# Transformer block: GpSimd's order written out in the input stages, with three steps of the input work moved

## The chip, the cores and the metric

The kernel runs on one core of a Trainium2 chip. Its time is the device time of one execution in microseconds; lower is better. The core has five engines that run their own instruction streams and wait for each other by semaphores: TensorE (PE in the profile; its weight loads are PEld), VectorE (DVE), ScalarE (ACT), GpSimd (POOL) and SyncE (SP, which here only issues DMAs). Everything is in 32-bit floats.

## The reference

One block of a conditioned transformer (DiT) on x of 2 batches x 2048 tokens x 576 features, 16 heads of 36 features, hidden width 2304:

```
mod = silu(c) @ w_ada + b_ada                 # six rows of 576 a batch
xn  = ln(x) * (1 + sc_msa) + sh_msa
q, k, v = split(xn @ w_qkv + b_qkv)           # by head
q, k = ln(q) * qn_g + qn_b, ln(k) * kn_g + kn_b      # over a head's 36 features
x   = x + g_msa * (softmax(q k^T / 6) v @ w_proj + b_proj)
xn2 = ln(x) * (1 + sc_mlp) + sh_mlp
out = x + g_mlp * (gelu(xn2 @ w1 + b1) @ w2 + b2)
```

## The kernel before, in words

The work is in stages. For each batch: the input stage (`inputs`, q, k and v of 16 tiles of 128 tokens), attention (`attend`, 8 pairs of heads x 4 blocks of 512 queries x 4 groups of keys), and the output product (`outputs`). Then the two products of the MLP for both batches.

**Order.** The program is traced once, and a planner gives each engine an order: of the instructions that its own timing model takes for ready, the one that was written first goes first. Inside `tc.manual_schedule(engines=...)` the named engines keep the order in which the code is written. TensorE is fixed throughout; in `inputs`, VectorE and SyncE are fixed, GpSimd and ScalarE are not. Each engine then runs its order strictly: an instruction that waits holds up all behind it, and on GpSimd this includes the DMAs that it issues.

**One token tile t on its way.** Its rows are loaded into one of three buffers (`tile_loaded`, L980, a DMA on GpSimd's queue), normed on VectorE (`rows_normed`; one step, the standard deviation L276, is on ScalarE) and transposed in 32x32 squares (L996); four DMAs on GpSimd's queue (L1001) write these to DRAM so that they lie by feature. Three DMAs on GpSimd's queue (L1009 once, L1011 twice) read the tile back by feature into `xnt`, which has three buffers: tile t+2 takes the one that tile t-1 had, so TensorE must have finished with it. ScalarE scales and shifts it (L1018 four times for the first 512 features; L388 and L389 for the last 64). L388 writes the last chunk rounded to the short matmul format, L389 writes it in full to the buffer `tail`, and GpSimd subtracts one from the other (L390). I call that subtraction **the remainder of tile t**. A product takes the 576 columns in two halves; of each, four full chunks come first (L1098, eight rows in the profile, since a 32-bit matmul is two instructions) and then the two parts of the last chunk (L1100). So a tile's first product waits for the remainder at its second L1100, some 2 us after it has begun.

**After the products.** `biased` (L1112 for q and k, L1115 for v) adds the bias from PSUM; `squared` (L1051, ScalarE) and `head_scale` (reduction L1056 and reciprocal L1061 on VectorE, square root L1059 on ScalarE, the scaling L1063 `both` on GpSimd) norm q and k by head. `by_feature(t)` transposes a tile's q and k in squares (L1076) and writes them with four DMAs of SyncE (L1078) to DRAM. `take_k_block` reads k of four tiles back for the first pair of heads (L812, L814, SyncE), and L847, L856, L857 on VectorE make `km` and `ke` of it for attention.

**The loop of `inputs`.** Step t calls, in the order of the code: `begun(t)` (loads the rows of tile t+4 and the features of tile t+2), the products of q and k, `turned_ahead(t)` (norms tile t+3 and writes its squares), `head_scale(t - 1)`, the product of v, `by_feature(t - 2)`, `squared(t)`, and `modulated_ahead(t)` (L1018 to L390 for tile t+1). In batch 0, tiles 0, 1 and 2 come another way before the loop (`first_modulated`, and transposes on TensorE in `second_by_feature`), their q and v products come before the loop too, and there `bias_made` centres the bias by head, writes it to DRAM (L955, GpSimd) and reads it back spread over 128 partitions (L956, GpSimd). Tile 15 is worked after the loop.

`s` tiles (PSUM, two banks each) are four, so a product may stand three products long before its bias is added.

Of the kernel before, what the change touches and what calls it, by code (L numbers as in the profile page):

```python
# [8 lines left out]
F32 = mybir.dt.float32  # L9
# [7 lines left out]
P = 128  # L17
# [14 lines left out]
def dit_block(  # L32
# [25 lines left out]
    nc = tc.nc  # L58
# [315 lines left out]
    def part_tiles(pool, cols, **bufs):  # L374

        return (
            pool.tile([P, FULL, cols], F32, name="xnt", **bufs),
            pool.tile([P, 2, cols], F32R, name="xnt4", **bufs),
            pool.tile([P, P], F32, name="tail", bufs=1),
        )  # L380

    def affine(which, k, b):
# [369 lines left out]
    def block_of_small():  # L752
# [163 lines left out]
        def first_weights(then):  # L916

            pool, (wq, wq4, bq), close = weight_tiles()
            raw = pool.tile([64, 3 * C], F32, name="raw_rows")

            def columns(f0, n):
                f = slice(f0, f0 + n)
                nc.sync.dma_start(out=wq[:, :, f], in_=w_qkv[0:512, f].rearrange("(k p) f -> p k f", p=P))

            columns(2 * C, HALF)
            nc.sync.dma_start(out=raw, in_=w_qkv[512:576, :])
            columns(2 * C + HALF, HALF)
            then(1)
            columns(0, HALF)
            then(2)  # L930
            columns(HALF, HALF)
            nc.sync.dma_start(out=bq[:, 2 * C :], in_=b_qkv[2 * C :].partition_broadcast(P))
            columns(C, HALF)
            columns(C + HALF, HALF)

            def made(w):
                for a in range(2):
                    centred(wq[:, :, w * C + a * HALF : w * C + (a + 1) * HALF])

            def ends_made(w):  # L940
                part = slice(w * C, (w + 1) * C)
                if w < 2:
                    centred(raw[:, part].unsqueeze(1))
                weight_parts(wq4[:, part], raw[:, part])

            by_head = pool.tile([2 * H, HD], F32, name="by_head")
            nc.gpsimd.dma_start(out=by_head, in_=b_qkv[0 : 2 * C].rearrange("(h d) -> h d", d=HD))

            def bias_made():
                mean = pool.tile([2 * H, 1], F32, name="mean")  # L950
                nc.vector.tensor_reduce(mean, by_head, AX.X, ALU.add)
                nc.vector.tensor_scalar_mul(mean, mean, 1.0 / HD)
                nc.vector.tensor_scalar(by_head, by_head, mean, None, ALU.subtract)
                saved["bq"] = dram.tile([2 * C], F32, name="bq_kept")
                nc.gpsimd.dma_start(out=saved["bq"].rearrange("(h d) -> h d", d=HD), in_=by_head)  # L955
                nc.gpsimd.dma_start(out=bq[:, 0 : 2 * C], in_=saved["bq"].partition_broadcast(P))  # L956

            def kept():
                saved["wq"] = dram.tile([P, FULL, 2 * C], F32, name="wq_kept")
                saved["wq4"] = dram.tile([P, 3 * C], F32, name="wq4_kept")  # L960
                nc.sync.dma_start(out=saved["wq"], in_=wq[:, :, 0 : 2 * C])
                nc.sync.dma_start(out=saved["wq4"], in_=wq4.bitcast(F32))

            return (wq, wq4, bq), close, (made, ends_made, bias_made, kept)

        def kept_weights():
            _, (wq, wq4, bq), close = weight_tiles()
# [62 lines left out]
        def second_by_feature(rows):  # L1030
            xnt = part_tiles(xs["pool"], P, bufs=3)
            t4, t1 = transposed(*rows)
            modulated_parts(xnt, slice(0, P), t4, t1[:, :P], 0, 0)
            return xnt
# [6 lines left out]
        def inputs(b, weights, making, work, xnts, turned, loaded):  # L1041

            wq, wq4, bq = weights
# [22 lines left out]
            by_square = qk_rows["dram"].rearrange("(k d) (t g j) -> t g d k j", d=SQ, g=P // SQ, j=SQ)  # L1066
            NSQ = C // SQ

            def by_feature(t, w0=0, w1=2, ready=True):

                begun = [*taken] if ready else []
                if ready:
                    taken.clear()
                part = slice(w0 * C, w1 * C)
                turned_qk = work.tile([P, 2 * C], F32, name="turned_qk", bufs=3)
                nc.vector.transpose(turned_qk[:, part], both[t][:, part])  # L1076
                for g in range(P // SQ):
                    nc.sync.dma_start(  # L1078
                        out=by_square[t, g][:, w0 * NSQ : w1 * NSQ, :],
                        in_=turned_qk[g * SQ : (g + 1) * SQ, part].rearrange("p (k j) -> p k j", j=SQ),  # L1080
                    )
                for do in begun:
                    do()
                if t == TPB - 1 and w0 == 0:
                    taken.extend(take_q(0, 0))
                if t + 1 in key_tiles and w1 == 2:
                    i = key_tiles.index(t + 1)
                    taken.append(take_k_block(*key_tiles[i - 1 : i + 1]))

            def product(w, t, ps=None, steps=(0, 1)):  # L1090

                ps = ps or s_tile()
                full, parts, _ = xnts[t]
                for a in range(2):
                    f = slice(w * C + a * HALF, w * C + (a + 1) * HALF)
                    out_a = ps[:, a, :HALF]
                    for k in range(FULL) if 0 in steps else ():
                        nc.tensor.matmul(out_a, full[:, k, :], wq[:, k, f], start=k == 0, stop=False)  # L1098
                    for i in range(2) if 1 in steps else ():
                        nc.tensor.matmul(out_a, parts[:, i, :], wq4[:, f], start=False, stop=i == 1)  # L1100
                return ps
# [20 lines left out]
            def begun(t):  # L1122
                if t + 4 < NT:
                    loaded[t + 4] = tile_loaded(x[b, (t + 4) * P : (t + 5) * P, :], nc.gpsimd)
                if t + 2 < NT and t + 2 not in xnts:
                    xnts[t + 2] = input_loaded(turned.pop(t + 2), nc.gpsimd)

            def turned_ahead(t):
                if t + 3 in loaded:
                    turned[t + 3] = tile_turned(loaded.pop(t + 3), nc.gpsimd)  # L1130

            def modulated_ahead(t):
                if t + 1 < NT and t + 1 not in modulated:
                    input_modulated(b, xnts[t + 1])
# [1 line left out]
            modulated = {0}  # L1136
            done = 0
            if b == 0:
                made, ends_made, bias_made, kept = making
                done, modulated = 3, {0, 1, 2}  # L1140
                ends_made(2)
                rows = {t: tile_normed(loaded.pop(t)) for t in (1, 2)}
                chosen = rows_chosen(work)
                bias_made()
                v = two_steps(2, 0)
                biased(2, v, 0)
                made(0)
                xnts[1] = second_by_feature(rows[1])
                v = product(2, 1)
                biased(2, v, 1)  # L1150
                ends_made(0)
                xnts[2] = second_by_feature(rows[2])
                v = product(2, 2)
                biased(2, v, 2)
                gains_by_row(chosen)
                turned_ahead(0)
                made(1)
                ends_made(1)
                for t in range(done):
                    q = two_steps(0, t) if t == 0 else product(0, t)  # L1160
                    biased(0, q, t)

            for t in range(NT - 1):
                begun(t)
                if t >= done:
                    q = product(0, t)
                k = product(1, t) if t >= done else two_steps(1, t)
                if t >= done:
                    biased(0, q, t)
                turned_ahead(t)  # L1170
                biased(1, k, t)
                if t > 0:
                    head_scale(t - 1)
                if t >= done:
                    v = product(2, t)
                    biased(2, v, t)
                if b == 0 and t == TPB + 1:
                    kept()
                if t >= 2:
                    by_feature(t - 2)  # L1180
                squared(t)
                modulated_ahead(t)

            t = NT - 1
            k, q, v = (product(w, t) for w in (1, 0, 2))
# [5 lines left out]
            by_feature(t - 1)  # L1191
            biased(0, q, t)
            squared(t, 0, 1)
            by_feature(t, 1, 2)
            head_scale(t, 0, 1)
            biased(2, v, t)
            by_feature(t, 0, 1, ready=False)
# [220 lines left out]
        weights, close_weights, making = first_weights(row_loaded)  # L1418
        row_loaded(3, nc.gpsimd)
        for b in range(B):  # L1420
            work, close_work = opened("work", side="right")
            with tc.manual_schedule(engines={mybir.EngineType.DVE, mybir.EngineType.SP}):
                left = inputs(b, weights, making, work, xnts, turned, loaded)
            close_weights()
            close_work()
# [464 lines left out]
```

## Time and profile before

| | |
|---|---|
| median of 3 runs | 3172.99 us (3171.32 to 3174.12) |
| the profiled execution: its time, its span | 3172.15 us, 3170.4 us |
| granted TensorE clock, mean | 0.996 |
| TensorE busy | 3129.0 us of the span (99%) |
| VectorE, ScalarE, GpSimd busy | 1513.7, 1471.7, 660.8 us |
| input stage of batch 0 on TensorE | 19.2 to 247.8 us |
| input stage of batch 1 on TensorE | 1106.7 to 1319.8 us |
| one step of the input stage on TensorE (87.58 to 100.81) | 13.23 us |

In a timeline's row stand the start and the length in us, the engine, the line, the operation, out<-in and the number of instructions that the row merges; in brackets the idle time of the engine before it and what ended that. A DMA's row on POOL is the time that GpSimd takes to issue it; the landing comes later. "PE x <- y" in a list of waits is who waited for whom: us in total, times, longest. In the chain of work that ended last, a DMA's row lasts from its issue to its landing, and SPq is SyncE's time to issue.

### The profile page before, as it was taken

Reading aid. Unit: us, or ns where it says so; the run is one execution under the profiler, and the core shown is the slowest. Engines: PE = TensorE matmul, PEld = TensorE weight load, DVE = VectorE, ACT = ScalarE, POOL = GpSimd, SP = SyncE. Lnnn points to the kernel's source line nnn. Section 1 sums busy time; section 2 is a strip of 40 time slices with the busy share of each in tenths; the row PEclk is TensorE's granted clock in tenths of the full one; section 3 lists DMA queues with packets and bytes.
Section 4 is the critical chain, followed back from the end, with each engine's and each line's share of the span. In section 5 each row is a group of like instructions: output and inputs, shape, how many; then the busy total and the mean of one; then the engine's idle time right before and its main releaser. Section 6 shows DMA issues by size and latency. Waiting matters only on the chain.

```text
span 3170.4 us, 46708 instructions
## 1 busy us (share of the span) xinstructions
PE 3129.0 (99%) x17553; PEld 1863.7 (59%) x17553; DVE 1513.7 (48%) x2173; ACT 1471.7 (46%) x2843; POOL 660.8 (21%) x924
## 2 busy tenths in 40 slices
PE   7999999999999999999999999999999999999999
PEld 5874333333333787633333333358888888777777
DVE  6653344444444556433444344345566554445454
ACT  2225666666666122366666666643565552000000
POOL 4541000111110455300001111012333320112121
PEclk9999999999999999999999999999999999999999
DMA  5654211222221745511122212246545434333331
GB/s 157 148 110 99 76 45 55 67 73 75 69 69 44 216 109 117 99 44 37 42 56 76 78 58 74 59 143 196 162 133 138 132 109 158 117 121 112 120 105 39
DMA packets 304531, 311.94 MB, mean 98 GB/s; under 512 B 183464, under 2 KB 237096, under 8 KB 302184
## 3 DMA queue, kind: packets, MB, share of 16 engines
q1 hardware_dynamic: 256704, 192.78, 21.3%
q0 software_dynamic: 44048, 110.48, 13.4%
q10 hardware_dynamic: 3544, 5.60, 0.5%
q8 instruction: 141, 2.31, 0.3%
q14 instruction: 94, 0.77, 0.1%
HBM read 191.80 MB, written 106.45 MB: 94 GB/s over the span
## 4 chain that ended last, share of the span: by engine, by line
PE 89%; DMA 2%; DVE 1%; issue 1%; POOL 1%; SPq 1%; ACT 0%; POOLq 0%; DVEq 0%; ACTq 0%
PE b L1233 29%; PE b L1220 19%; PE s L1802 15%; PE m L1642 11%; PE s L1098 6%; PE s L406 3%; PE m L1656 2%; PE one L1642 2%; PE s L1100 1%; DMA qk<-turned_qk 0%; PE s L417 0%; DMA ke<-qk 0%; DMA xnt<-turned 0%; POOL both L1063 0%; SPq L1078 0%
## 5 line engine op out<-in xcount | busy, mean ns | idle before, releaser
L1224 ACT ACTIVATE pt<-b 128x512 f32<-128x512 f32 x2048 | 1057.4, 610 | 490.6 <-PE b L1233 278.9
L1233 PE MATMUL b<-pt,vt 128*64 128x512 f32 x4096 | 937.0, 599 | 0.0
L1233 PEld LDWEIGHTS b<-pt,vt 128*64 128x64 f32 x4096 | 272.3, 137 | 584.7 <-issue 442.5
L1220 PE MATMUL b<-qm,km 32*128 32x512 f32 x4096 | 572.1, 616 | 2.8 <-issue 2.5
L1283 DVE TENSOR_TENSOR ot<-b,ot 128x512 f32<-128x512 f32 x192 | 132.8, 692 | 628.3 <-PE b L1233 628.3
L1220 PE MATMUL b<-qe,ke 16*128 16x512 f32 x2048 | 423.7, 792 | 2.1 <-DVE ke L857 2.1
L1098 PE MATMUL s<-wq,xnt 128*128 128x288 f32 x1536 | 405.3, 407 | 2.5 <-ACT xnt L395 2.1
L1220 PEld LDWEIGHTS b<-qm,km 32*128 32x128 f32 x4096 | 192.1, 185 | 277.4 <-ACT pt L1224 211.2
L1802 PE MATMUL s<-ws,as 128*128 128x288 f32 x1440 | 351.8, 406 | 0.0
L1098 PEld LDWEIGHTS s<-wq,xnt 128*128 128x128 f32 x1536 | 281.8, 190 | 65.3 <-ACT xnt L395 1.6
L1802 PEld LDWEIGHTS s<-ws,as 128*128 128x128 f32 x1440 | 273.6, 190 | 75.6
L1252 DVE RECIPROCAL den<-den 128x512 f32<-128x512 f32 x64 | 213.6, 3337 | 9.7 <-DMA den<-den_dram 9.7
L1642 PE MATMUL m<-xnt,wb 128*128 128x256 f32 x864 | 210.3, 379 | 2.1 <-DVE cs L1676 1.2
L1642 PE MATMUL m<-s,wb 128*128 128x256 f32 x864 | 210.0, 379 | 0.0
L1001 POOL DMA_DIRECT2D turned<-squares x212 | 142.7, 679 | 256.2 <-DVE squares L996 234.7
L1281 DVE COPY ot<-b 128x512 f32<-128x512 f32 x64 | 44.3, 692 | 281.6 <-PE b L1233 281.6
L1220 PEld LDWEIGHTS b<-qe,ke 16*128 16x128 f32 x2048 | 107.9, 185 | 118.2 <-issue 112.8
L1642 PEld LDWEIGHTS m<-s,wb 128*128 128x128 f32 x864 | 164.2, 190 | 22.3
L1642 PEld LDWEIGHTS m<-xnt,wb 128*128 128x128 f32 x864 | 158.9, 190 | 21.6 <-DVE cs L1676 1.4
L1680 ACT ACTIVATE cs<-cs,b_sb 128x512 f32<-128x512 f32 x144 | 98.9, 719 | 112.2 <-DVE cs L1675 86.2
L812 POOL DMA_DIRECT2D km<-qk x56 | 27.9, 499 | 582.1 <-PE b L1220 573.5
L1018 ACT ACTIVATE xnt<-xnt,mod 128x128 f32<-128x128 f32 x244 | 100.4, 481 | 96.8 <-DMA xnt<-turned 96.8
(204 smaller groups left out, 2937.0 us busy)
## 6 DMA issues: line engine op xcount, KB each, us to landing
gelu<-cs SPq DMA_DIRECT2D x144, 256.0 KB
hidden<-gelu SPq DMA_DIRECT2D x16, 2304.0 KB
x_dram<-spare POOLq DMA_DIRECT2D x64, 288.0 KB, 2.5
qk<-turned_qk SPq DMA_DIRECT2D x120, 144.0 KB
qm<-qk SPq DMA_DIRECT2D x256, 64.0 KB
den<-den_dram SPq DMA_DIRECT2D x128, 128.0 KB
turned<-squares POOLq DMA_DIRECT2D x212, 72.0 KB, 2.5
xnt<-turned POOLq DMA_DIRECT2D x54, 256.0 KB, 3.9
```

Of the source, the lines that this page charges most:

```text
L406: nc.tensor.matmul(outs[a], stationary(k, a), moving(k, a), start=(first and k == 0), stop=(not first and k == FULL - 1),)
L1001: queue.dma_start(out=by_square[g], in_=squares[g * SQ : (g + 1) * SQ, :].rearrange("p (k j) -> p k j", j=SQ))
L1018: nc.scalar.activation(part, part, AF.Identity, **affine(which, k, b))
L1098: nc.tensor.matmul(out_a, full[:, k, :], wq[:, k, f], start=k == 0, stop=False)
L1220: nc.tensor.matmul(ps, k[r, keys], q[r, :], start=first, stop=not first)
L1224: nc.scalar.activation(pt[:, h, :], banks[2 * c + h], AF.Exp, scale=SCALE)
L1233: nc.tensor.matmul(acc[64 * h : 64 * h + 64, :], vt[:, v0 : v0 + 64], pt[:, h, :], start=pt is pts[0][0], stop=pt is pts[-1][0],)
L1252: nc.vector.reciprocal(den, den)
L1283: nc.vector.tensor_tensor(ot, acc, ot, ALU.add)
L1642: nc.tensor.matmul(out_m[m], wb[:, slot[m], k, f * P : (f + 1) * P], moving[m](k), start=k == 0 and m in (1, 2, 5, 6), stop=k == 1 and m == 1,
L1680: nc.scalar.activation(part, part, AF.Gelu, bias=b1_sb[:, g : g + 1])
L1802: nc.tensor.matmul(ms[m], stationary[m][:, f, :], ws[m][:, f, :], start=(f == 0), stop=(f == HF - 1))
```

## The change

1. GpSimd joins the engines whose order is fixed in `inputs`, so its instructions and DMAs run as the code is written.
2. `modulated_ahead(t)` is called right after `begun(t)`, no longer at the end of the step. `tail` gets two buffers.
3. In batch 0, step 0 also calls `turned_ahead(1)`, which norms tile 4 (the fifth); that was in step 1.
4. The spreading DMA of the bias (L956) moves out of `bias_made` into `bias_spread`, which is called after the remainder of tile 2.
5. The k of tile 15 is written to DRAM by GpSimd's queue (`queue=nc.gpsimd`), no longer by SyncE's.

```diff
@@ part_tiles
-            pool.tile([P, P], F32, name="tail", bufs=1),
+            pool.tile([P, P], F32, name="tail", bufs=2),
@@ first_weights, bias_made
                 nc.gpsimd.dma_start(out=saved["bq"].rearrange("(h d) -> h d", d=HD), in_=by_head)
+
+            def bias_spread():
                 nc.gpsimd.dma_start(out=bq[:, 0 : 2 * C], in_=saved["bq"].partition_broadcast(P))
...
-            return (wq, wq4, bq), close, (made, ends_made, bias_made, kept)
+            return (wq, wq4, bq), close, (made, ends_made, bias_made, bias_spread, kept)
@@ inputs
-            def by_feature(t, w0=0, w1=2, ready=True):
+            def by_feature(t, w0=0, w1=2, ready=True, queue=nc.sync):
...
-                    nc.sync.dma_start(
+                    queue.dma_start(
                         out=by_square[t, g][:, w0 * NSQ : w1 * NSQ, :],
...
-                made, ends_made, bias_made, kept = making
+                made, ends_made, bias_made, bias_spread, kept = making
...
                 xnts[2] = second_by_feature(rows[2])
+                bias_spread()
                 v = product(2, 2)
...
             for t in range(NT - 1):
                 begun(t)
+                modulated_ahead(t)
                 if t >= done:
                     q = product(0, t)
                 k = product(1, t) if t >= done else two_steps(1, t)
                 if t >= done:
                     biased(0, q, t)
                 turned_ahead(t)
+                if b == 0 and t == 0:
+                    turned_ahead(t + 1)
                 biased(1, k, t)
...
                 squared(t)
-                modulated_ahead(t)
...
             squared(t, 0, 1)
-            by_feature(t, 1, 2)
+            by_feature(t, 1, 2, queue=nc.gpsimd)
             head_scale(t, 0, 1)
@@ the loop over batches
-            with tc.manual_schedule(engines={mybir.EngineType.DVE, mybir.EngineType.SP}):
+            with tc.manual_schedule(
+                engines={mybir.EngineType.DVE, mybir.EngineType.SP, mybir.EngineType.Pool}
+            ):
                 left = inputs(b, weights, making, work, xnts, turned, loaded)
```

## The prediction

> **What bounds the kernel.** First the busy times (part 1 of the page), then TensorE's waits, then the timelines around the longest ones.
>
> ```profile
> PE 3129.0 (99%) x17553; PEld 1863.7 (59%) x17553; DVE 1513.7 (48%) x2173; ACT 1471.7 (46%) x2843; POOL 660.8 (21%) x924
> ```
>
> TensorE sets the time, and the change leaves all its matmuls. So it can only win idle TensorE time, 41.4 us of the span (3170.4 - 3129.0), and what idling costs afterwards. TensorE's waits say where it is:
>
> ```profile
> PE s L1100 <- POOL xnt L390: 10.5, 5, 7.1
> PE s L306 <- DVE x_first L283: 9.8, 1, 9.8
> PE s L417 <- DVE product L1357: 2.5, 1, 2.5
> PE b L1220 <- DVE ke L857: 2.1, 2, 1.4
> ```
>
> The first row is the remainder, five times late. The second is the start of the program, which the change does not touch. The fourth is the start of attention, twice. The longest wait, in TensorE's timeline:
>
> ```profile
> 65.06 2.10 PE L1098 MATMUL s<-wq,xnt 128*128 128x288 f32 x8
> 66.79 0.51 PE L1100 MATMUL s<-wq,xnt 128*128 128x288 f32 x1
> 74.41 0.61 PE L1100 MATMUL s<-wq,xnt 128*128 128x288 f32 x1 [7.11 <-POOL xnt L390]
> 74.81 3.84 PE L1098 MATMUL s<-wq,xnt 128*128 128x288 f32 x8
> ```
>
> It is the first q product of the loop, tile 3's. Eight matmuls took 2.10 us before the wait and 3.84 after it. The granted clock (after PEclk's place in each row, the third number from the end) tells why:
>
> ```profile
> 74.00:76.00 2.00, 1.59 (x4) 1.31 (x5) 0.00 (x0) 0.49 (x1) 0.98 (x3) 0.50 1.05 162
> 76.00:78.00 2.00, 2.00 (x5) 1.43 (x5) 0.00 (x0) 0.00 (x0) 1.99 (x4) 0.50 0.99 213
> 78.00:80.00 2.00, 2.00 (x10) 1.54 (x10) 1.04 (x2) 0.00 (x0) 0.71 (x2) 0.92 0.87 221
> ```
>
> Tile 3's products began at 65.06 and a step is 13.23 us, so tile 4's were due at 78.29. They began at 87.58. **This one wait costs 9.3 us**: 7.4 of waiting (67.03 to 74.41) and 1.9 at half clock.
>
> What GpSimd did meanwhile:
>
> ```profile
> 60.50 2.69 POOL L1001 DMA_DIRECT2D turned<-squares  x4 [2.48 <-DVE squares L996]
> 63.70 2.12 POOL L1063 TENSOR_TENSOR both<-both,inv 128x1152 f32<-128x1152 f32 x1 [0.51 <-DVE inv L1061]
> 67.25 0.69 POOL L1001 DMA_DIRECT2D turned<-squares  x1 [1.43 <-DVE squares L996]
> 69.77 2.03 POOL L1001 DMA_DIRECT2D turned<-squares  x3
> 71.81 2.14 POOL L1063 TENSOR_TENSOR both<-both,inv 128x1152 f32<-128x1152 f32 x1
> 73.90 0.46 POOL L390 TENSOR_TENSOR xnt<-tail,xnt 128x128 fp32r<-128x128 f32 x1
> ```
>
> ScalarE had finished `tail` of tile 3 at 61.92. The remainder, 0.46 us of work, then stood 12 us behind tile 5's squares, tile 4's loads (67.93 to 69.77) and two scalings.
>
> **1, 2, 3: GpSimd's order, worked through for batch 0.** In the order of the code GpSimd now runs: four square DMAs of tile 3 (43.02 to 45.68, as before), rows of tile 4 (before at 25.87, now behind these: issued 45.7, landing within 3.4 to 5.8 as other such loads, by 51.5). VectorE is free at 53.93 after the three q biases and norms tile 4 there; the same chain took 57.12 to 60.21, so squares stand at 57.0 (before 60.2) and the bias of k of tile 0 waits 0.6 us (56.44 to 57.0), hidden by the four `s` tiles. GpSimd issues them 57.0 to 59.7, rows of tile 5 to 60.3, three feature loads of tile 3 (0.76 + 1.07) to 62.1, which were at 56.18; they land 3.2 us after their issue at best, so 63.6. ScalarE needs 59.49 to 61.92, 2.4 us, for a tile: 66.0. Meanwhile k of tile 1 leaves TensorE as before, its bias add starts at 60.86, reduction, square root and reciprocal end at 63.61, and `both` of tile 0 runs 63.70 to 65.82. Then rows of tile 6 (0.6), features of tile 4 (1.83), and the remainder of tile 3 (0.45): **68.70** in place of 74.36. TensorE is there at 67.03 and now waits 1.7 us.
>
> Does that shorter wait also cost the clock? After 1.13 us of waiting (the row at 170.32) the next eight matmuls took 2.10 us; after 7.1 the clock halved; nothing in between is in this trace. The Trainium skill (TensorE: Matmul & The Clock Gate, "Part 1: The HAM clock gate") halves it after about 3.4 us without work. By that rule 1.7 us cost nothing more, by the nearest row above them they would cost up to 1.9. I take nothing, since 1.7 is nearer to 1.13. Gain so far 9.3 - 1.7 = 7.6.
>
> **4 and a loss early.** The DMA that writes the centred bias (L955) must wait for VectorE (28.70) and was at 28.99 to 29.51, behind the remainder of tile 1 (28.22). Now it is ahead: the remainder ends at 29.97, and TensorE, which went on at 28.72, goes on at 30.02, +1.3. Everything behind shifts, also the remainder of tile 2. That one took 1.48 us (34.19 to 35.67) beside a VectorE product of two SBUF operands (33.99 to 35.35); at 35.5 that is over and 0.45 should do, so TensorE's 0.96 us of waiting there falls away. Net loss 0.34, at worst 1.4. The spreading DMA, now at 36 in place of 32.85, takes 4.3 to land and is read at 51.84; without these 11 us of cover each us late would be one lost. VectorE's work of 28 to 52 is not moved. **Sum of 1 to 4 up to tile 4: 7.6 - 0.34 = 7.2.**
>
> **The later steps.** Two waits of 1.13 and 1.05 us (tile 10 of both batches) have the same cause, the remainder behind squares and scaling; in the new order it comes 3.4 us into a step, after `begun`'s four DMAs, and is needed 13.23 + 2.2 us into it. Cover 12 us, gain 2.2. What is queued behind a waiting GpSimd: the feature load of tile t+2 waits for tile t+2's squares to land. Where `kept` stores 3.2 MB (107.24), squares issued at 109.41 to 111.43 landed only at 122.9. There the remainder of tile 7 will stand behind the load of tile 8 and come 11.5 us into step 6, needed at 15.4: covered by 3.9. With `tail` double, ScalarE's next one need not wait for the remainder (1076.57, released by it): the deviation behind it is 0.6 earlier, and TensorE's wait of 2.46 us (L417) hangs on that. I take 0.5.
>
> **5, the start of attention.** TensorE's third group of scores waits for `ke` of the last four tiles. The chain:
>
> ```profile
> 249.95 1.01 SPq L1078
> 252.15 3.75 DMA qk<-turned_qk
> 257.40 4.63 DMA ke<-qk
> 264.04 2.93 PE b L1220 x12
> ```
>
> VectorE had k of tile 15 ready at 247.87; SyncE, busy with tile 14, issued it at 249.92 to 252.66. GpSimd is idle and needs 4 x 0.67: 247.9 to 250.6, the last 2.3 us earlier. Behind it: the scaling of q of tile 15 slides from 249.40 to 250.6 and the key loads of pair 1 by as much; both are needed many steps later. But the Trainium skill (DMA: Bandwidth & Descriptors, "Issuing engines are not separate DMA queues") says that all queues end on the same 16 engines and a second one saves only issue time, which speaks against these 2.3 us. The packet records agree with it here: 1000 to 1200 writes of 128 bytes a us without a gap from 243.4 to 252. Tiles 13, 14 and k of 15 are 11,520 such writes, at 1,080 a us done at 254.1, landed by 254.9; they landed at 255.89. So 1.0, not 2.3. In batch 1 SyncE lost more (1318.84 to 1326.28, landed 1329.36); there the limit is 1326.3 + 0.8, but three loads of qm stood ahead of k's until 1328.24, so 1.1 of 2.3. The key loads now fall onto the same DMA engines: -0.4. Taken **1.7**, between 0 and 6 (if the clock, 0.66 in 264 to 272, also stays up).
>
> **Sum**: 7.2 + 2.2 + 0.5 + 1.7 = 11.6. From the profiled execution, 3172.15 (span 3170.4 and 1.75 around it), 3160.6; the median is 0.84 higher, so **3161.4**. A change of 0.2% (6.3 us) is about what a measurement can tell from none.
>
> **Rivals.** (B) *ScalarE's planned order gives most of it back.* Before, the planner put tile 3's L1018 (59.49) ahead of the first square root (62.91). If it does so again, the root waits for features that land at 63.6: root 66.5, `both` to 69.4, remainder 72.3. The wait is 5.0 us and the clock falls too: gain 2.1 in place of 7.2, time 3166.5. For: at 127.80 ScalarE stood 7.1 us idle in just such an order. Against: now the loads are issued 4 us later, the root is not. (C) *Attention's start gains fully*, clock included: 4.2 more, 3157. For: the `ke` wait and the halved clock lie together. Against: the saturated engines. (D) *Slower.* ScalarE runs the scaling of the next tile, now written early in a step, ahead of roots and deviations in every step and waits for its load; VectorE's order is fixed, so the bias adds wait behind. With four `s` tiles a product may wait 3 x 4.41 = 13.2 us; the worst such stop now, 5.4 us (125.1 to 130.5), cost nothing. From 13.2 us on each further us costs 24 us over the steps of both batches; 0.8 more and the time is 3180. (E) *It does nothing*: the remainder waits for something else. Against it: `tail` was done 12 us before. Then 3172.
>
> **Chances.** Forecast 0.45 (3159 to 3165), B 0.27, C 0.12, D 0.10, E 0.06. B straddles the bound of 0.2%, so half of it counts as faster: faster 0.45 + 0.12 + 0.13 = 0.70; same 0.14 + 0.06 = 0.20; slower 0.10. Range 3157 to 3170: from C to B with the early loss at 1.4 and no gain in attention (3166.5 + 1.1 + 1.7); D and E lie outside.
>
> **What would show it.** Right: tile 3's remainder at about 68.7 with a wait of 1 to 2 us and clock 1.0 behind it; tile 4's products 7 us earlier; no wait for L390 after that; tile 1's remainder after L955, with +1.3 us at 28.7; k of 15 landed 1 us sooner. Wrong: ScalarE's L1018 of tile 3 ahead of its first square root, a wait of 5 us; waits for L1112's `s` tiles; a new wait near tile 7 or in the output product of batch 0, where GpSimd already stood 9.5 us for tile 1's remainder (1076.09).

## The result, and the profile after

| | before | changed |
|---|---|---|
| median, us (8 runs each) | 3172.35 (3171.32 to 3174.12) | 3161.99 (3159.22 to 3164.09) |
| ratio, 95% interval | | 0.9967 [0.9956, 0.9978] |
| profiled execution: time, span, us | 3172.15, 3170.4 | 3161.52, 3159.7 |
| granted TensorE clock, mean | 0.996 | 0.998 |

The change is faster, by 10.4 us or 0.33%. The forecast was 3161.4 us. The sum of its terms came out nearly as written; two of the terms did not, and the experiments show why.

The busy times of the changed kernel and TensorE's waits (who waited <- for whom: us in total, times, longest):

```profile
PE 3125.0 (99%) x17553; PEld 1860.9 (59%) x17553; DVE 1513.1 (48%) x2173; ACT 1470.5 (47%) x2843; POOL 666.7 (21%) x932
```

```profile
PE s L1102 <- POOL xnt L390: 3.0, 2, 1.5
PE b L1225 <- DVE km L847: 2.3, 1, 2.3
PE b L1225 <- DVE ke L857: 2.1, 2, 1.4
...
PE s L406 <- DVE product L1362: 1.5, 1, 1.5
...
PE s L417 <- DVE product L1362: 1.0, 1, 1.0
```

(L1100 and L1102 are the L1098 and L1100 of before, L1225 the L1220, L1362 the L1357.) The remainder is late twice instead of five times, 3.0 us instead of 10.5. A second wait in the output product, 1.5 us, is new. The `km` row, at the start of attention in batch 1, is a wait that the kernel before had too, 1.49 us long and put down to "issue"; the kernel before stands first:

```profile
1334.17 1.19 PE L1220 MATMUL b<-qm,km 32*128 32x512 f32 x2 [1.49 <-issue]
```

```profile
1323.41 0.79 PE L1225 MATMUL b<-qm,km 32*128 32x512 f32 x2 [2.32 <-DVE km L847]
```

TensorE is busy 4.0 us less with the same matmuls: that is clock.

Both kernels run the same 17,553 matmuls in the same order, so the start of the same matmul can be compared in the two profiled executions. What follows is that comparison: at each place, how much TensorE gained on the kernel before.

| place | forecast, us | measured, us |
|---|---|---|
| start of the program (not touched) | 0 | -0.64 |
| tile 1's remainder | -1.3 | -1.24 |
| tile 2's remainder | +0.96 | +1.02 |
| tile 3's remainder, with the clock behind it | +7.6 | +7.57 (5.66 and 1.91) |
| tile 10's remainder, both batches | +2.2 | +2.72 (1.40 and 1.32) |
| output product of batch 0 | +0.5 | +1.15 |
| start of attention, batch 0 | +1.0 | +0.99 |
| start of attention, batch 1 | +1.1 | -1.23 |
| collision of the key loads, both batches | -0.4 | in the two rows above |
| MLP (not touched) | 0 | +0.17 |
| end | +11.6 | +10.5 |

The long wait is gone. TensorE's timeline at tile 3, and the granted clock (third number from the end of the row):

```profile
67.64 0.51 PE L1102 MATMUL s<-wq,xnt 128*128 128x288 f32 x1
69.60 0.40 PE L1102 MATMUL s<-wq,xnt 128*128 128x288 f32 x1 [1.45 <-POOL xnt L390]
69.84 2.10 PE L1100 MATMUL s<-wq,xnt 128*128 128x288 f32 x8
```

```profile
70.00:72.00 2.00, 2.00 (x10) 1.58 (x10) 1.15 (x1) 0.90 (x3) 2.00 (x4) 1.00 0.59 115
```

1.45 us where 7.11 stood, and eight matmuls behind it in 2.10 us, not 3.84: no clock was lost. GpSimd's timeline ahead of it, where the idle time that a row waited out stands in brackets:

```profile
57.75 2.65 POOL L1003 DMA_DIRECT2D turned<-squares  x4 [10.95 <-DVE squares L998]
60.39 0.58 POOL L982 DMA_DIRECT2D xt<-in_x_dram  x1
60.96 0.76 POOL L1011 DMA_DIRECT2D xnt<-turned  x1
61.71 1.10 POOL L1013 DMA_DIRECT2D xnt<-turned  x2
64.55 2.12 POOL L1065 TENSOR_TENSOR both<-both,inv 128x1152 f32<-128x1152 f32 x1 [1.74 <-DVE inv L1063]
66.62 0.59 POOL L982 DMA_DIRECT2D x_first<-in_x_dram  x1
67.21 0.77 POOL L1011 DMA_DIRECT2D xnt<-turned  x1
67.96 1.10 POOL L1013 DMA_DIRECT2D xnt<-turned  x2
69.08 0.47 POOL L390 TENSOR_TENSOR xnt<-tail,xnt 128x128 fp32r<-128x128 f32 x1
```

This is the forecast's list row by row. Its remainder ended at 68.70; here it ends at 69.55, and 0.85 us of that is what the start of the program (0.64) and the two early remainders (0.21) had already cost.

### The profile page after: what moved, and what is told of

Same layout as the page of the kernel before. It is cut to its first block, busy times and chain, and to the rows that moved or that the text cites. A ratio compares the mean times of both kernels' runs of the same rounds, so it can differ in the third digit from the quotient of the medians.

```text
span 3159.7 us, 46700 instructions
## 1 busy us (share of the span) xinstructions
PE 3125.0 (99%) x17553; PEld 1860.9 (59%) x17553; DVE 1513.1 (48%) x2173; ACT 1470.5 (47%) x2843; POOL 666.7 (21%) x932
## 4 chain that ended last, share of the span: by engine, by line
PE 94%; DMA 2%; DVE 1%; issue 1%; SPq 1%; POOL 0%; ACT 0%; DVEq 0%; POOLq 0%; ACTq 0%
PE b L1238 29%; PE b L1225 19%; PE s L1809 15%; PE m L1649 11%; PE s L1100 11%; PE s L406 3%; PE m L1663 2%; PE one L1649 2%; PE s L1102 2%; DMA qk<-turned_qk 0%; DMA xt<-in_x_dram 0%; DMA ke<-qk 0%; PE s L417 0%; DMA xnt<-turned 0%; DVE turned_qk L1078 0%
## 5 line engine op out<-in xcount | busy, mean ns | idle before, releaser
L1225 PE MATMUL b<-qm,km 32*128 32x512 f32 x4096 | 570.4, 615 | 3.6 <-DVE km L847 2.3
L1225 PE MATMUL b<-qe,ke 16*128 16x512 f32 x2048 | 422.8, 791 | 2.1 <-DVE ke L857 2.1
L1100 PE MATMUL s<-wq,xnt 128*128 128x288 f32 x1536 | 403.5, 406 | 2.8 <-ACT xnt L395 2.0
L1225 PEld LDWEIGHTS b<-qm,km 32*128 32x128 f32 x4096 | 191.7, 185 | 278.3 <-ACT pt L1229 211.2
L1100 PEld LDWEIGHTS s<-wq,xnt 128*128 128x128 f32 x1536 | 280.6, 190 | 65.1 <-ACT xnt L395 1.6
L1225 PEld LDWEIGHTS b<-qe,ke 16*128 16x128 f32 x2048 | 107.5, 184 | 117.3 <-issue 112.8
L1342 POOL DMA_DIRECT2D spare<-in_x_dram x32 | 17.4, 545 | 599.7 <-DVE met L791 599.7
```

The costliest lines, as they stand in the source:

```text
L1225: nc.tensor.matmul(ps, k[r, keys], q[r, :], start=first, stop=not first)
```

## The experiments

Every time is a median; the interval is that of the ratio to the kernel before, which ran beside each. The intervals are about 4 us wide to each side, so what is under 4 us is read from the traces, matmul against matmul as above, and only supported by the medians.

| kernel | median, us | ratio to before [95%] |
|---|---|---|
| changed kernel | 3161.99 | 0.9967 [0.9956, 0.9978] |
| without the early scaling (part 2) | 3201.22 | 1.0084 [1.0063, 1.0106] |
| GpSimd's order free (no part 1) | 3160.91 | 0.9962 [0.9948, 0.9976] |
| tile 4 normed late (no part 3) | 3161.48 | 0.9961 [0.9947, 0.9975] |
| bias DMAs together (no part 4) | 3164.84 | 0.9971 [0.9961, 0.9982] |
| k of tile 15 by SyncE (no part 5) | 3161.76 | 0.9962 [0.9948, 0.9976] |
| `tail` single | 3162.71 | 0.9965 [0.9951, 0.9979] |
| before, with the early scaling alone | 3162.28 | 0.9968 [0.9955, 0.9980] |
| changed, keys of pair 1 held | 3156.55 | 0.9948 [0.9931, 0.9964] |
| the same, k of tile 15 by SyncE | 3157.27 | 0.9950 [0.9937, 0.9964] |
| changed, keys held and two moves | 3154.09 | 0.9939 [0.9925, 0.9952] |
| before, early scaling and keys held | 3155.34 | 0.9944 [0.9930, 0.9958] |

### Which part carries the gain at tile 3

The theory at this point was that of the prediction, that parts 1 to 3 together bring the remainder forward. Three kernels undo them one at a time.

**The call of part 2 put back to the end of the step, GpSimd's order still fixed:**

```diff
             for t in range(NT - 1):
                 begun(t)
-                modulated_ahead(t)
...
                 squared(t)
+                modulated_ahead(t)
```

> The changed kernel with the call of part 2 put back: the next tile is scaled at the end of the step, GpSimd's order stays fixed. Theory 'the early call carries the gain': the remainder of tile 3 stands behind tile 5's squares and two scalings again, a wait of 7.4 us with 1.9 of clock behind it, so 7.5 slower at tile 4, and waits of about 1.1 at tile 10 of both batches come back: 3162.0 + 9.7 = 3171.7, at least 3169.5. Rival 'the fixed order carries it': not more than 1 us slower, 3163.

Measured: 3201.22 us, 39 slower than the changed kernel and 28 slower than the kernel before. The direction is that of the first theory, the size is four times what it gave. TensorE's waits:

```profile
PE s L1102 <- POOL xnt L390: 30.9, 21, 6.7
```

Tile 3 is late about as expected (6.66 us), but the remainder is late 21 times in all. GpSimd's timeline near the end of batch 1's input stage, and ScalarE's beside it:

```profile
1291.92 0.46 POOL L390 TENSOR_TENSOR xnt<-tail,xnt 128x128 fp32r<-128x128 f32 x1
1292.32 0.60 POOL L982 DMA_DIRECT2D x_first<-x_dram  x1
1293.22 0.75 POOL L1011 DMA_DIRECT2D xnt<-turned  x1 [0.30 <-issue]
1293.96 1.08 POOL L1013 DMA_DIRECT2D xnt<-turned  x2
1302.80 2.69 POOL L1003 DMA_DIRECT2D turned<-squares  x4 [7.76 <-DVE squares L998]
1305.50 2.14 POOL L1065 TENSOR_TENSOR both<-both,inv 128x1152 f32<-128x1152 f32 x1
1307.59 0.46 POOL L390 TENSOR_TENSOR xnt<-tail,xnt 128x128 fp32r<-128x128 f32 x1
```

```profile
1298.27 1.65 ACT L1020 ACTIVATE xnt<-xnt,mod 128x128 f32<-128x128 f32 x4 [8.12 <-DMA xnt<-turned]
1299.83 0.48 ACT L388 ACTIVATE xnt<-xnt,mod 128x128 fp32r<-128x128 f32 x1
1300.21 0.48 ACT L389 ACTIVATE tail<-xnt,mod 128x128 f32<-128x128 f32 x1
1300.60 0.28 ACT L276 ACTIVATE std<-mv,eps 128x1 f32<-128x1 f32 x1
```

The rows close a ring. The feature loads (1293.22) stand behind the remainder (1291.92). ScalarE waits for them (1298.27), and in its queue the standard deviation of a later tile (1300.60) stands behind the scaling. VectorE's norm needs that deviation, GpSimd needs the norm for the squares (1302.80, after 7.76 us of idling), and the next remainder stands behind these, 7 us after its input `tail` was written. Once round takes 15.7 us (1291.92 to 1307.59), and a step was 13.23. So **a fixed order with the remainder last is worse than the planner's**, which took the remainder whenever its input was there. The change's two halves are not alike: the early call is what frees TensorE, and the fixed order by itself only takes freedom away.

**GpSimd's order left to the planner, all else as in the changed kernel:**

```diff
-            with tc.manual_schedule(
-                engines={mybir.EngineType.DVE, mybir.EngineType.SP, mybir.EngineType.Pool}
-            ):
+            with tc.manual_schedule(engines={mybir.EngineType.DVE, mybir.EngineType.SP}):
                 left = inputs(b, weights, making, work, xnts, turned, loaded)
```

> The changed kernel with part 1 undone alone: GpSimd's order is the planner's again, all else stays. The planner's list has tile 3's remainder right behind the first scaling, ahead of tile 6's rows and tile 4's features, and tile 1's remainder ahead of the bias write, but the spreading DMA of the bias ahead of tile 2's remainder. Theory 'the early call carries the gain': TensorE's wait at tile 3 falls from 1.45 to 0 to 0.5, at tile 1 from 1.5 to 0.3, at tile 2 it rises to about 1; 3160 to 3163. Rival 'the fixed order carries it': waits of 5 us or more come back in the input stages, 3169 or above.

Measured: 3160.91 us, within the first theory. The remainder of tile 3 follows the scaling directly, at 66.71 to 67.37, ahead of tile 6's rows and tile 4's features, and TensorE doesn't wait for it; it waits 0.27 us for tile 1's and 0.83 for tile 2's. By tile 4 this kernel has gained 2.05 us on the changed one (the start of the program left out), and about as much is left at the end of the profiled execution. Part 1 gains nothing there; it costs about 2 us, too little for the medians to show.

**Tile 4 normed in step 1 again:**

```diff
                 turned_ahead(t)
-                if b == 0 and t == 0:
-                    turned_ahead(t + 1)
```

> The changed kernel with part 3 undone: tile 4 is normed in step 1 again. GpSimd's fixed order then has the rows of tile 5 and the features of tile 3 ahead of tile 4's squares. Theory 'the order alone frees the remainder': squares of tile 4 issued 61 to 64, the feature load of tile 4 waits for their landing (66 to 66.5) and ends at about 68.3, the remainder of tile 3 ends at about 68.8 to 69.5: the wait stays at 1.5 us, no clock is lost, the time at 3162 within 1. Rival 'the early norm carries it': everything on GpSimd up to the remainder comes 3.2 us later (norm at 57.1 in place of 53.9), the wait is 4.7, the clock falls for 1.9 us: 3162 + 3.2 + 1.9 = 3167.

Measured: 3161.48 us, and the wait at tile 3 is 1.43 us, as in the changed kernel. The squares of tile 4 were issued 4.1 us later (61.85), but without them GpSimd had the feature load of tile 3 done by 59.4, so the first scaling (65.05), not the squares, set the remainder in both. Part 3 is worth nothing.

**The kernel before, with the early call alone:**

```diff
             for t in range(NT - 1):
                 begun(t)
+                modulated_ahead(t)
...
                 squared(t)
-                modulated_ahead(t)
```

> The kernel before with one edit: the next tile is scaled right after the step's loads, not at the end of the step. GpSimd's order is the planner's, tail is single, parts 3, 4 and 5 are left out. Theory 'the early call carries the whole gain': the remainder of tile 3 follows the first scaling directly and ends at about 66.4, no wait at 67.0, the clock holds, the waits at tile 10 are gone, tile 1 and 2 wait as before (0.3 and 1.0), attention and output product as before: 3172.9 - 9.3 - 2.2 = 3161.4. Rival 'the other parts carry a good share': 3166 or above.

Measured: 3162.28 us. GpSimd's timeline:

```profile
64.28 2.12 POOL L1063 TENSOR_TENSOR both<-both,inv 128x1152 f32<-128x1152 f32 x1 [0.51 <-DVE inv L1061]
66.36 0.66 POOL L390 TENSOR_TENSOR xnt<-tail,xnt 128x128 fp32r<-128x128 f32 x1
```

TensorE passes tile 3 without a wait and gains 9.3 us there on the kernel before, and tile 10 of both batches gives 2.7 more. One moved line carries the whole of the gain; the planner does the rest, since of what it takes for ready it picks what was written first.

### The bias DMAs

```diff
                 nc.gpsimd.dma_start(out=saved["bq"].rearrange("(h d) -> h d", d=HD), in_=by_head)
-
-            def bias_spread():
                 nc.gpsimd.dma_start(out=bq[:, 0 : 2 * C], in_=saved["bq"].partition_broadcast(P))
...
-            return (wq, wq4, bq), close, (made, ends_made, bias_made, bias_spread, kept)
+            return (wq, wq4, bq), close, (made, ends_made, bias_made, lambda: None, kept)
```

> The changed kernel with part 4 undone: the spreading DMA of the bias stands right behind the bias write again, now in GpSimd's fixed order and so ahead of the remainders of tiles 1 and 2. Theory 'a DMA that waits holds up all behind it on GpSimd': it waits for the landing of the bias write (issued at 29.5, some 3.3 us), is issued at 33.4 to 33.9, the remainder of tile 1 ends at 34.4, TensorE waits 5.3 us in place of 1.5 and the clock falls behind it: 3.8 to 5.7 slower, 3166 to 3168. Rival 'it is hidden': 3162 within 1.

Measured: 3164.84 us, 2.85 above the changed kernel. GpSimd's and TensorE's timelines (L1098 and L1100 are the products' lines here, as in the kernel before):

```profile
29.43 0.51 POOL L955 DMA_DIRECT2D bq_kept<-by_head  x1 [6.56 <-DVE by_head L953]
32.18 0.57 POOL L956 DMA_DIRECT2D bq<-bq_kept  x1 [2.23 <-DMA bq_kept<-by_head]
32.77 0.47 POOL L390 TENSOR_TENSOR xnt<-tail,xnt 128x128 fp32r<-128x128 f32 x1
```

```profile
33.30 0.61 PE L1100 MATMUL s<-wq,xnt 128*128 128x288 f32 x1 [4.31 <-POOL xnt L390]
33.70 4.04 PE L1098 MATMUL s<-wq,xnt 128*128 128x288 f32 x8
```

The mechanism is that of the first theory: GpSimd idles 2.23 us on the landing of its own write, the remainder stands behind that, and the clock halves after the wait of 4.31. Matmul against matmul the loss is 2.7, then 5.0 behind the clock, and 5.7 after tile 2, which is the size expected. By the end of the profiled execution 3.8 of it was left; 1.9 came back at the two starts of attention, where the clock differs from run to run. So up to tile 2 the fixed order costs 0.2 us against the kernel before with part 4, and 6.0 without: the part undoes a loss that part 1 would have brought.

### The second `tail`

```diff
-            pool.tile([P, P], F32, name="tail", bufs=2),
+            pool.tile([P, P], F32, name="tail", bufs=1),
```

> The changed kernel with tail single again. The prediction put the second tail at 0.5 us, all of it at the output product of batch 0; between the two traces TensorE won 1.4 to 1.6 us there (its wait at L417 fell from 2.46 to 1.03, and the clock behind it held). If the buffer is the cause, the second L389 waits for the remainder again, the standard deviation comes 0.5 us later, the wait at L417 is 2.4 with a lower clock: 3162.0 + 1.5 = 3163.5. Rival 'the shorter wait comes from how loads fell in time, the buffer gives 0.5 at most': the wait at L417 grows by 0.5 or less, 3162.0 to 3162.5. In both no new wait for the remainder in the input stages.

Measured: 3162.71 us, and in the trace a wait of 2.19 us at L417, with the granted clock at 0.50 from 1070 to 1072. ScalarE's second L389 stood 0.57 us for the remainder, as before, and the deviation behind it came later by that; but the features, too, reached ScalarE 0.5 us later here, so of the 1.16 us by which the wait is longer the buffer explains about half. Over the whole output product this kernel loses 0.9 us. That is not idle time: with two tails TensorE waits 1.03 and then 1.47, with one it waits 2.19 once. The total hardly moves; what is saved is the half clock behind the longer wait. It isn't saved each time: in the kernel with the k of tile 15 on SyncE and two tails, the second wait was 1.89 and the clock did fall, which took 1.7 us. And the kernel before with the early call alone, whose `tail` is single, gained 1.11 us in the output product, where the changed kernel gained 1.15. So no run shows that this gain needs the buffer; where the waits fall in the clock's grid (last section) decides as much.

### The start of attention

**Part 5 undone:**

```diff
-            by_feature(t, 1, 2, queue=nc.gpsimd)
+            by_feature(t, 1, 2)
```

> The changed kernel with part 5 undone: the k of tile 15 is again written by SyncE in both batches. The prediction's term says part 5 is worth 1.7 us (between 0 and 6): 3162.0 + 1.7 = 3163.7, slower in both batches. Rival, read from the two traces: in batch 0 TensorE won 1.1 us over the start of attention (its lead went from 8.0 to 9.1 us), in batch 1 it lost 1.1 (11.5 to 10.4), because the key loads that now started 2 us sooner took 6.8 us in place of 4.0. By that the undone part costs 1.1 in batch 0, gives 1.1 back in batch 1, and the time stays at 3162.0 within 0.5.

Measured: 3161.76 us; in the traces part 5 undone costs 1.05 us in batch 0 and gives 1.26 back in batch 1. The rival holds: part 5 gains nothing. The chain of work at the start of attention in batch 1, ahead of the third group of scores (start, length, what; a DMA's row lasts from its issue to its landing), in the kernel before, in the changed kernel and with part 5 undone:

```profile
1325.50 3.84 DMA qk<-turned_qk
...
1330.93 3.94 DMA ke<-qk
```

```profile
1317.35 6.01 DMA ke<-qk
...
1325.37 2.92 PE b L1225 x10
```

```profile
1322.43 3.94 DMA ke<-qk
```

(The 6.8 and 4.0 us of the expectation run from the issue of the first of the four key loads to the landing of `km`; the rows here are the last load.) Counted from the start of attention's products, the load starts 2.0 us earlier in the changed kernel than before, and lasts 2.07 longer. What ran beside it? GpSimd loads the keys of the second pair of heads in eight DMAs, four for each half of the tokens. In the changed kernel the first four were issued from 1312.67 to 1314.90 and landed between 1316.86 and 1319.88, into the time of SyncE's key loads from 1315.82 on. In the kernel before they had landed by 1328.47, before SyncE's began at 1329.42. The other four, which need tile 15, were issued beside SyncE's loads in both kernels (1329.90 to 1332.07 before, 1316.29 to 1318.45 here).

**The keys of the second pair held:** GpSimd's loads for pair 1 now wait until the first values are copied to `ot`, because one element of `ot` is first copied into `km` and multiplied with one of `ke`, the tiles that they fill.

```diff
-                if g == 1 and qb == 0 and p + 1 < NPAIR:
+                if g == (2 if p == 0 else 1) and qb == 0 and p + 1 < NPAIR:
...
                         nc.vector.tensor_copy(ot, acc)
+                        if (bp, bqb) == (0, 0):
+                            nc.vector.tensor_copy(km[1][0:1, 0:1], ot[0:1, 0:1])
+                            nc.vector.tensor_tensor(met, ke[1][0:1, 0:1], ot[0:1, 0:1], ALU.mult)
```

> The changed kernel, in which the key loads of the second pair of heads, which GpSimd issues some 4.5 us into attention, are held until the first values are copied to ot (about 12 us in); they are needed some 90 us later. It tells why part 5 gave nothing in batch 1, where the key loads of SyncE took 6.8 us with GpSimd's write and 4.0 without. Theory 'GpSimd's loads for the second pair now run beside them': the loads take 4 us again in batch 1, TensorE's wait for km falls from 2.3 to below 0.5, a gain of 2 us there and 0 to 1 in batch 0: 3159 to 3160. Rival 'the writes of k and q of tile 15 themselves slow them': the loads still take 6 us or more, no gain, 3162.

Measured: 3156.55 us, 5.4 below the changed kernel and more than the first theory gave. Matmul against matmul it is 2.9 us in batch 0 and 3.8 in batch 1. The chain in batch 1:

```profile
1313.41 3.61 PE b L1238 x16
...
1317.05 0.70 DVE ot L1286
...
1318.01 0.55 DVE km L847
...
1320.39 2.08 PE b L1225 x14
```

No DMA is in it any more. With none of GpSimd's loads beside it, the last of SyncE's key loads landed 2.26 us after its issue (1314.54 to 1316.80, by the updates of its semaphore), where it took 6.01 beside all eight and 3.94 beside four. The writes of k and q of tile 15 are there as before, so the rival falls. From the products through the copy to `ot` and `km` it is all computing, and TensorE's two waits there are 0.61 and 0.51 us instead of 2.32 and 0.75. In batch 0 the granted clock stayed at 1.00 over the 8 us from 256, where it was 0.79 in the changed kernel and 0.66 in the kernel before (from 264); that is the part the theory had not counted. So the loads of the second pair were the cause of the longer waits, in both batches, and had been there in the kernel before too. Over both batches the waits are 3.2 us shorter than in the changed kernel; the rest of the gain is clock, and that part is not steady. In the traces of the four kernels with held keys the two waits are always the same (0.61 to 0.63 and 0.51 to 0.52 us), yet over these eight starts of attention the clock was halved for 6.83 us twice, for 3.41 us three times, and three times not at all.

**With the keys held, part 5 undone:**

```diff
-            by_feature(t, 1, 2, queue=nc.gpsimd)
+            by_feature(t, 1, 2)
...   (and the edit above)
```

> The changed kernel with the key loads of the second pair held, and the k of tile 15 written by SyncE again in both batches. With the loads out of the way it tells what part 5 itself is worth. Theory 'the earlier landing is worth what was forecast, once nothing collides': between the traces k of tile 15 landed, after the start of attention, 0.3 us sooner in batch 0 and 2.1 in batch 1 with GpSimd's write; so 2 to 3 us slower than with the loads held and GpSimd writing: 3158.5 to 3159.5. Rival 'the queue makes no difference': 3156.5 within 0.5.

Measured: 3157.27 us; from the first products on, the two traces stay within 0.6 us of each other. The first theory falls: the chain of work is the same one, over `ot`, so a write that lands sooner has nobody who waits for it.

### Versions that beat both

**Keys held, and two moves:** the bias write goes behind tile 2's remainder too, and in step 2 of batch 0 the scaling is called ahead of the loads.

```diff
             def bias_spread():
+                nc.gpsimd.dma_start(out=saved["bq"].rearrange("(h d) -> h d", d=HD), in_=by_head)
                 nc.gpsimd.dma_start(out=bq[:, 0 : 2 * C], in_=saved["bq"].partition_broadcast(P))
...
-                begun(t)
-                modulated_ahead(t)
+                if b == 0 and t == 2:
+                    modulated_ahead(t)
+                    begun(t)
+                else:
+                    begun(t)
+                    modulated_ahead(t)
```

> The changed kernel with three edits: the key loads of the second pair of heads held as in the run before; the bias write moved behind the remainder of tile 2, beside the spreading DMA; in step 2 of batch 0 alone the scaling of tile 3 called ahead of the step's loads, so that the remainder of tile 3 stands directly behind the first scaling. Theory: the wait at tile 1 falls from 1.5 to 0.3, that at tile 3 from 1.45 to 0, and with the held loads 3156.55 - 1.25 - 1.45 = 3153.9. Rival 'the moved work comes late': the bias is not there for the first k product at 52, or tile 4's features, now issued 0.5 later, make tile 4 wait; then 3156 or above.

Measured: 3154.09 us, the lowest median of all. It meets the number, but the trace gives only part of it: the wait at tile 3 is gone (1.33 us gained), and that at tile 1 nearly (1.23), but tile 2's is back at 0.84, its remainder beside VectorE's work again. So the two moves gain 1.7 us of the 2.7, and the rest of the difference between the medians is within what they can tell. The profiled execution itself, 3158.05, was the slowest of its five: the clock was halved for 6.83 us at both starts of attention. The bias and tile 4's features came in time.

**The kernel before, with two edits alone,** the early call and the held keys:

```diff
                 begun(t)
+                modulated_ahead(t)
...
-                modulated_ahead(t)
...   (and the keys held, as above)
```

> The kernel before with two edits: the scaling of the next tile called right after the step's loads, and the key loads of the second pair of heads held until the first values are copied. Theory 'the two are independent, and nothing else of the change is needed': the first alone gave 3162.28, the held loads took 5.4 us off the changed kernel (3161.99 to 3156.55), so 3156.9. Rival 'the held loads only help where GpSimd writes the k of tile 15': 3160 or above.

Measured: 3155.34 us. The gains of the two edits add up within the noise, and with them nothing else of the change shows in the time: its difference to 3154.09 is within what these runs can tell.

## Why the prediction was right, and which terms were not

- **Tile 3, -7.6 us: right.** By the forecast's count TensorE stood ready for 1.72 us (67.88 to 69.60; 1.7 forecast; the profile's 1.45 begins at the modelled end of the matmul before), the clock held, and 7.57 were gained. The working put it down to parts 1, 2 and 3 together; the runs show that the early call alone carries it, that the early norm has no share, and that the fixed order takes 1.7 us of it away, since it puts two loads ahead of the remainder that the planner puts behind it.
- **The early loss, +0.34: right.** +1.24 and -1.02 make 0.2. Tile 2's remainder took 0.46 us where it had taken 1.48 beside VectorE's product.
- **Tile 10, -2.2: right** (2.72).
- **The output product, -0.5: right in its sign, wrong in its mechanism.** The deviation did come earlier and L417 waited 1.4 us less, but the next product waited 1.47 more. The 1.15 us are clock.
- **The start of attention, -1.7: failed.** It measured +0.24 over both batches. The step that failed is "the key loads now fall onto the same DMA engines: -0.4". In batch 1 that collision cost 2.07 us on the last load, five times the term, and it ate the 2.0 us that were won ahead of it: TensorE's waits there grew from 2.16 us to 3.07, and the rest of the 1.23 lost is clock. The prediction named GpSimd's key loads of pair 1 only as "needed many steps later". They were; but an early transfer that nobody needs takes the DMA engines from a late one that TensorE waits for. What it cited of the Trainium skill (DMA: Bandwidth & Descriptors, "Issuing engines are not separate DMA queues") spoke against a gain from a second queue, and the runs agree as to the time: 3161.99 by GpSimd and 3161.76 by SyncE. (With the keys held, where nobody waits for the landing, it is 3156.55 and 3157.27.)
- **The start of the program, +0.64:** not forecast; no part of the change lies ahead of it. 0.30 of it is a longer wait for a load of weights (`wq`).

The forecast sum of 11.6 against 10.5 is thus 1.9 too much in attention and 0.6 at the start, against 0.65 too little in the output product, 0.5 at tile 10, 0.2 in the MLP and 0.1 in the early loss; the errors in part cancelled, which is why the total fits better than its terms.

**The rivals.** B fell on its own row: ScalarE's first square root is at 63.76, ahead of tile 3's scaling at 65.04. C needed attention to gain fully; the changed kernel gained nothing there, but the mechanism was real, since the held keys give 5.4 us, the clock included. D's mechanism did not show in the changed kernel: no wait for the bias adds. A relative of it did, in the kernel without the early call, where loads, scaling, deviation and squares wait for each other in a ring, at 39 us. E fell with tile 3.

**The clock after a wait** was the open choice of the prediction: nothing for 1.7 us, by the nearest row; also nothing by the rule of the Trainium skill (TensorE: Matmul & The Clock Gate, "Part 1: The HAM clock gate"), an idle window of about 3.4 us. The choice was right, and it was closer than the rule makes it look, as the last section shows: a wait of 1.87 us has cost the clock.

## What to carry to other kernels

When one engine computes and issues DMAs in strict order, look for the short operation that a busier engine waits for, and write it ahead of what merely prepares later work; a planner that prefers what is written first may need nothing more. Fix an order by hand only together with such a move: a wrong fixed order can close a ring through several queues and stretch every step (39 us here), where the planner's order had lost 10.5 us in five waits. And ask of each early transfer that nobody needs yet what it runs beside: holding one group back by 8 us took 5.4 us off the median, half as much as the whole change.

## What the runs showed of the hardware

**The clock can fall after waits well below 3.4 us.** TensorE's timeline without the early call, three waits (in brackets) and the eight matmuls behind each:

```profile
136.23 0.40 PE L1102 MATMUL s<-wq,xnt 128*128 128x288 f32 x1 [3.36 <-POOL xnt L390]
136.47 3.45 PE L1100 MATMUL s<-wq,xnt 128*128 128x288 f32 x8
...
211.19 0.40 PE L1102 MATMUL s<-wq,xnt 128*128 128x288 f32 x1 [1.87 <-POOL xnt L390]
211.42 3.31 PE L1100 MATMUL s<-wq,xnt 128*128 128x288 f32 x8
...
1308.10 0.40 PE L1102 MATMUL s<-wq,xnt 128*128 128x288 f32 x1 [2.17 <-POOL xnt L390]
1308.34 2.10 PE L1100 MATMUL s<-wq,xnt 128*128 128x288 f32 x8
```

After 1.87 us the eight matmuls took 3.31, after 2.17 they took 2.10. Over all the traces, in the products of the input and output stages from 25 us on: after waits of up to 1.67 us the clock never fell; of the nine between 1.78 and 2.46 us it fell after four (1.87, 1.89, 2.19, 2.46) and held after five (1.78, 1.93, 2.09, 2.17, 2.26); from 3.36 on (3.36, 4.31, 6.66, 7.11) it fell each time. By the rule's 3.4 us none of the four should have cost anything; here the measurement decides.

**What decides it is where the wait lies.** By the clock records of all 13 traces, the granted clock changes only at points that lie whole multiples of 3.413 us apart. In the kernel before it fell at 71.50, 262.65, 1078.43 and 1334.43 us, the last three 56, 295 and 370 such steps after the first, and it stayed at half for one step or two (3.41 or 6.83 us). So a wait that a point divides puts less idle time into one step:

| wait, us | most idle time in one step, us | clock |
|---|---|---|
| 1.78 | 1.78 | held |
| 1.93 | 1.45 | held |
| 2.09 | 1.67 | held |
| 2.17 | 1.91 | held |
| 2.26 | 1.72 | held |
| 1.87 | 1.87 | fell |
| 1.89 | 1.89 | fell |
| 2.19 | 2.19 | fell |
| 2.46 | 2.46 | fell |
| 3.36 | 2.58 | fell |
| 4.31 | 2.76 | fell |

From about 1.9 us of idle time in one step on the clock fell; 1.87 and 1.91 stand the wrong way round, and with matmul ends that are modelled this can't be told finer. The points lie differently to the program's start in each execution, so a kernel can't choose them: a wait of about 2 us is a toss, worth 1.7 us in the output product of the kernel with part 5 undone. This count holds for the input and output stages. At the start of attention, where the matmuls use 32 and 16 rows, the clock fell with as little as 1.00 us of idle time in a step (the kernel before, at 262.65).
